# A graph network kernel whose adjacency-building stage takes its node blocks in another order

## The chip, the cores and the metric

The kernel runs on one core of one Trainium2 chip. The metric is device time in microseconds, as the median of several executions. The engines are TensorE (PE in the profile, with PEld its weight loads), VectorE (DVE), ScalarE (ACT), GpSimd (POOL) and SyncE (SP), which issues most of the DMAs.

## What is computed

A graph of 3125 nodes with 128 features and 100000 edges, sorted by destination, goes through four residual blocks, each followed by a layer norm. The last one distinguishes 8 types of edges (relations). Cut to what matters:

```
x = layernorm(x + gcn3(x))        # 3 layers: A-normalised sum over edges, W, layer norm, relu
x = layernorm(x + gcn1(x))        # sum over edges of x @ W.T + b
x = layernorm(x + gin(x))         # (1+eps)*x + sum over edges, two linear layers with batch norm
x = layernorm(x + rgcn2(x))       # 2 layers: per relation, mean over its edges, times W[r]

def rgcn_layer(x, src, dst, etype, W, W_root, b, num_rels):
    h = einsum('ni,rio->rno', x, W)
    msg = h[etype, src]
    seg = dst * num_rels + etype
    sums = segment_sum(msg, seg, N * num_rels)
    cnt = segment_sum(1, seg, N * num_rels)
    mean = sums / maximum(cnt, 1.0)
    return mean.reshape(N, num_rels, do).sum(axis=1) + x @ W_root + b
```

## The kernel before, in words

All sums over edges of the first three blocks are done as dense matrix products with the matrix of edge counts, 3200 x 3200, so the **first stage** builds this matrix from the list of edges. Everything after it uses the matrix. The nodes lie in 25 blocks of 128 (NB = 25), and two blocks make a superblock (SB = 13; the last one, 12, holds only block 24). For blocks 0 to 14 (ND = 15) the stage also builds one matrix of counts for each of the 8 relations, in bytes; for blocks 15 to 24 the last part of the kernel gathers rows by edge instead, so no such matrices are made. In what follows a block is *counted* if its relation matrices are built, and *plain* if not. Superblocks 0 to 6 are counted, 8 to 12 are plain, and superblock 7 holds counted block 14 and plain block 15.

The steps for a superblock s are, with the lines of the profile:

- `coarse` (L258): VectorE compares a sample of the destinations with the node numbers ("junk", L262), and makes row numbers ("crow", "irow", L265 and L266); POOL gathers two rows of the destinations ("g", L270).
- `search` (L277): VectorE counts in these ("junk", L281) and makes pointers into the list of edges ("ptr", L285).
- `fetch_edges` (L287): POOL gathers the edges of each node ("ew", L290).
- `keys` (L298): VectorE splits each edge into its fields ("f", "valid", "qf", "kb", "kq", L302 to L314), TensorE transposes the keys (L319) and ScalarE copies them to "kT" (L320).

For a block b, `total` (L344) goes through two halves. Each half makes one-hot matrices from kT on VectorE ("lo" and "hi", by the helper at L191), multiplies them on TensorE (L356) into the PSUM tile "bld", and ScalarE copies that to "at" (L359) in two copies. Between the halves stands `stored` of the block before. For a counted block each half goes on with `packed_counts` (L327): VectorE scales lo to "rlo" (L331) and makes "rhq" (L191); TensorE multiplies (L339), and ScalarE copies to "rb" in eight copies (L342). When both halves are done, eight DMAs store rb (L369, queue of SP).

`stored` (L375) adds the identity to at (VectorE, L376), stores it (adj_t, L377), transposes it on TensorE (L382), copies it to "av" on ScalarE in two copies (L383), stores that (adj, L384), and adds up degrees into "leave" on TensorE (L388), an accumulation that runs over all blocks.

The buffers lo, rlo, hi, rhq, at, rb and av exist twice each, ew three times, g six times; bld has two PSUM buffers.

The order of the work is written out in the loop at L404. The searches run ahead: while superblock s is built, between its two blocks, the keys of s + 1, the search and fetch of s + 2 and the coarse step of s + 3 are placed, and made to come after the last hi of the first block on VectorE (`behind`, L253). The framework gives each engine one list of instructions in a scheduled order: by the order of the program, but an instruction that is ready earlier can stand ahead of it. Each engine then runs its list in order.

```
for s in range(SB):
    built = total(2 * s, built)
    if s + 1 < SB:
        keys(s + 1, edges.pop(s + 1), last[0])
    if s + 2 < SB:
        search(s + 2, near.pop(s + 2), last[0])
        edges[s + 2] = fetch_edges(s + 2)
    if s + 3 < SB:
        near[s + 3] = coarse(s + 3, last[0])
    if 2 * s + 1 < NB:
        built = total(2 * s + 1, built)
stored(*built)
```

After the loop the degrees in leave become "dinv" (L424 to L438), and the **second stage** begins: x times dinv, split into two halves ("halves", L583 and L584), is multiplied with the matrix of counts. For each group of columns the matrix comes in five loads of five blocks each ("m", L594, queue of SP), is cast to "mf" by ACT (L611) or DVE (L613), and multiplied (L628). Beside this stage VectorE and POOL do small steps for the relations, among them a gather of edges ("gedge", L475).

The functions with their lines:

Of the kernel before, what the change touches and what calls it, by code (L numbers as in the profile page):

```python
# [24 lines left out]
NB = 25  # L25
# [20 lines left out]
def cols(m0, nb):  # L46
    return slice(m0 * P, (m0 + nb) * P)
# [8 lines left out]
SB = 13  # L56
# [3 lines left out]
ND = 15  # L60
# [13 lines left out]
def listed(ctx: ExitStack, tc: tile.TileContext, p: dict, out: bass.AP, bad):  # L74
# [92 lines left out]
    with tc.tile_pool(name="f_w", bufs=1) as wp, tc.tile_pool(name="f_bg", bufs=1) as bg:  # L167
# [28 lines left out]
        with tc.tile_pool(name="f_t1", bufs=1) as t1:  # L196
# [90 lines left out]
            def fetch_edges(s):  # L287
                ew = t1.tile([P, 2, SL], I32, name="ew", bufs=3)
                for i in range(2):
                    ld = nc.gpsimd.indirect_dma_start(  # L290
                        out=ew[:, i, :], out_offset=None, in_=pk[:],
                        in_offset=bass.IndirectOffsetOnAxis(ap=ptr[:, 2 * s + i : 2 * s + i + 1], axis=0),
                    )
                if s == 0:
                    packed.append(ld)
                return ew

# [77 lines left out]
            def stored(b, at):  # L375
                nc.vector.tensor_add(at[:, b, :], at[:, b, :], identb)  # L376
                nc.sync.dma_start(adj_t[b], at)  # L377
                av = t1.tile([P, NP], BF, name="av", bufs=2)
                for m0, nb in ((0, 13), (13, 12)):
                    t = psum.tile([P, 2048], BF, name="bld", tag="bld", bufs=2)  # L380
                    for k in range(nb):
                        nc.tensor.transpose(t[:, cols(k, 1)], at[:, m0 + k, :], identb)  # L382
                    nc.scalar.copy(av[:, cols(m0, nb)], t[:, : nb * P])  # L383
                nc.sync.dma_start(adj[b], av)  # L384
                for i in range(7):
                    w = min(512, NP - 512 * i)
                    q = 32 * (i % 4)
                    nc.tensor.matmul(leave[i // 4][q : q + 32, :w], onesb, av[:, 512 * i : 512 * i + w],  # L388
                                     start=(b == 0), stop=(b == NB - 1), skip_group_check=True)


            last = [None]
            near, edges = {}, {}
            built = None
            with tc.high_priority():
                near[0] = coarse(0)
                near[1] = coarse(1)
                search(0, near.pop(0))
                edges[0] = fetch_edges(0)
                key = keys(0, edges.pop(0))  # L400
            search(1, near.pop(1))
            edges[1] = fetch_edges(1)
            near[2] = coarse(2, key)
            for s in range(SB):  # L404
                built = total(2 * s, built)
                if s + 1 < SB:
                    keys(s + 1, edges.pop(s + 1), last[0])
                if s + 2 < SB:
                    search(s + 2, near.pop(s + 2), last[0])
                    edges[s + 2] = fetch_edges(s + 2)  # L410
                if s + 3 < SB:
                    near[s + 3] = coarse(s + 3, last[0])
                if 2 * s + 1 < NB:
                    built = total(2 * s + 1, built)
            stored(*built)

            tc.add_manual_dep(words.ins, started[0].ins.name, WAIT, reason="the search comes first")
# [336 lines left out]
    with until_end:  # L754
# [262 lines left out]
        with tc.tile_pool(name="f_hr", bufs=1, reuse_waits="tile") as hp:  # L1017
# [15 lines left out]
            for m0, nb in CH:  # L1033
                o = psum.tile([P, 512], F32, name="mi", tag="mi", bufs=2)
                for a in range(2):
                    nc.tensor.matmul(o[:, : nb * P], root2[:, a, :], hT[:, a, cols(m0, nb)],
                                     start=(a == 0), stop=(a == 1))
# [31 lines left out]
            for r in range(R):  # L1069
                nxt = None  # L1070
                for i, (m0, nb) in enumerate(DENSE):
                    inv = load_inv(r, m0, nb)
                    acc = relation(r, m0, nb, hr, work, 2.1, (1, 1, 1, 1, 1))
                    s = hp.tile([P, 512], F32, name="s", bufs=2)
# [628 lines left out]
```

## Time and profile before

| What | us |
|---|---|
| Time of three runs, median | 2020.77 (2017.62 to 2021.79) |
| Profiled execution | 2027.4 |
| its span, first to last instruction | 2025.5 |
| granted TensorE clock, mean | 0.975 |
| first lo of the first stage | 29.8 |
| last hi of the first stage | 389.1 |
| last av copy | 397.0 |
| first cast of the second stage | 404.35 |
| first product of the second stage | 407.85 |
| DVE busy, whole span | 1205.1 |
| ACT busy, whole span | 1253.0 |

The profile is one execution, recorded by the hardware. Its page cuts the span into 40 slices of 50.6 us and gives each engine's busy share in tenths. A *stretch* is the same between two times, in us. A *timeline* lists one engine's instructions: start, duration, engine, line, operation, output and inputs with their shapes, how often, and in brackets how long the engine had been idle and what released it. A *wait* names the engine and line that waited, and what for: us in total, how many times, and the longest. The profiled execution's own time is compared with its own sums; the median is of other executions.

### The profile page before, as it was taken

The numbers are of one execution on the slowest core, as the hardware profiler recorded it, in microseconds if no ns is written. First come the engines' busy times: TensorE is split into PE (matmuls) and PEld (weight loads), VectorE is DVE, ScalarE is ACT, GpSimd is POOL, SyncE is SP. The second block draws the span as 40 slices with busy tenths as digits, with TensorE's granted clock in tenths as the row PEclk, the third lists the DMA queues.
The fourth block names the chain that finished last, engine by engine and source line by source line (L and its number), as shares of the span: only waits on it lengthen the run. The fifth ranks groups of instructions, "written<-read, shape, count | busy, mean of one in ns | idle before, by whom it ended". The sixth has DMA issues, their size and how long they took to land.

```text
span 2025.5 us, 30183 instructions
## 1 busy us (share of the span) xinstructions
PE 1794.3 (89%) x11523; PEld 1387.0 (68%) x11523; DVE 1205.1 (59%) x2055; ACT 1253.0 (62%) x1118; POOL 859.5 (42%) x717
## 2 busy tenths in 40 slices
PE   2677676669999999889999999999999999999897
PEld 1555555458888888667577567758757777777676
DVE  6999998777768863475455345435346444434424
ACT  3999997757888666663233333233338777777774
POOL 5315624120000000027777267706716666666664
PEclk9999998889999999999999999999999999999998
DMA  4766776667888887477677457737659887888773
GB/s 100 277 271 266 291 287 237 247 189 232 255 259 257 251 268 235 140 225 190 177 212 207 148 171 209 188 101 198 184 151 269 243 228 220 235 240 245 196 204 101
DMA packets 398932, 435.67 MB, mean 215 GB/s; under 512 B 27166, under 2 KB 355838, under 8 KB 398776
## 3 DMA queue, kind: packets, MB, share of 16 engines
q1 hardware_dynamic: 346274, 336.92, 53.0%
q0 software_dynamic: 33632, 67.07, 12.9%
q10 hardware_dynamic: 18870, 29.66, 4.9%
q8 instruction: 92, 1.51, 0.3%
q14 instruction: 64, 0.52, 0.1%
HBM read 319.07 MB, written 114.46 MB: 214 GB/s over the span
## 4 chain that ended last, share of the span: by engine, by line
PE 57%; ACT 4%; issue 3%; DVE 3%; another core or an unknown queue 2%; DMA 1%; ACTq 0%; SPq 0%; DVEq 0%
PE acc L885 30%; PE acc L628 8%; PE x L927 8%; PE mi L962 4%; PE mi L975 4%; ACT m L767 3%; PE mi L966 1%; DMA back<-ht_d 1%; PE mi L650 0%; PE x L836 0%; PE mi L740 0%; DVE hilo L790 0%; ACT mf L611 0%; DVE f L1027 0%
## 5 line engine op out<-in xcount | busy, mean ns | idle before, releaser
L885 PE MATMUL acc<-m,hilo 128*128 128x512 f32 (+1 forms) x3200 | 792.3, 393 | 22.8 <-ACT m L767 10.8
L767 ACT CAST m<-m 128x2560 fp32r<-128x2560 uint8 (+1 forms) x225 | 486.8, 2196 | 372.5 <-PE acc L885 148.7
L885 PEld LDWEIGHTS acc<-m,hilo 128*128 128x128 f32 x3200 | 576.5, 190 | 130.3 <-issue 17.6
L919 POOL DMA_INDIRECT gx<-xt_d,gsrc x321 | 366.1, 1140 | 638.5 <-DVE z L1007 413.7
L919 POOL DMA_INDIRECT gx<-ht_d,gsrc x321 | 326.2, 1016 | 200.1 <-issue 72.0
L628 PE MATMUL acc<-mf,halves 128*128 128x512 f32 (+1 forms) x1750 | 383.9, 377 | 11.5 <-DVE mf L613 11.0
L628 PEld LDWEIGHTS acc<-mf,halves 128*128 128x128 f32 x1750 | 320.4, 190 | 60.4 <-DVE mf L613 11.9
L611 ACT CAST mf<-m 128x2560 fp32r<-128x2560 bf16 (+1 forms) x126 | 263.7, 2100 | 67.3 <-PE acc L628 34.8
L927 PE MATMUL x<-oh,gx 128*128 128x192 bf16 (+5 forms) x2208 | 227.1, 239 | 5.5 <-issue 5.2
L927 PEld LDWEIGHTS <-gx 128*128 128x128 bf16 x2208 | 157.0, 97 | 99.2 <-issue 89.6
L767 DVE CAST m<-m 128x2560 fp32r<-128x2560 uint8 (+1 forms) x95 | 158.5, 1670 | 110.6 <-issue 40.3
L909 DVE TENSOR_TENSOR oh<-iota,gkey 128x768 bf16<-128x768 bf16 (+1 forms) x170 | 90.3, 532 | 208.5 <-PE x L927 143.2
L342 ACT CAST rb<-bld 128x800 uint16<-128x800 f32 x240 | 180.0, 847 | 6.5 <-PE bld L339 6.5
L339 PE MATMUL bld<-rhq,rlo 128*128 128x200 bf16 x960 | 124.2, 253 | 49.4 <-ACT rb L342 36.5
L290 POOL DMA_INDIRECT ew<-pk,ptr x26 | 72.7, 2797 | 193.9 <-DVE ptr L285 189.6
L339 PEld LDWEIGHTS <-rlo 128*128 128x128 bf16 x960 | 86.9, 98 | 85.3 <-issue 80.9
L613 DVE CAST mf<-m 128x2560 fp32r<-128x2560 bf16 (+1 forms) x49 | 97.5, 1989 | 70.1 <-PE acc L628 69.9
L191 DVE TENSOR_TENSOR lo<-iota,kT 128x4096 bf16<-128x4096 bf16 x50 | 114.2, 2283 | 11.1 <-PE bld L356 11.1
L191 DVE TENSOR_TENSOR rhq<-iota,kT 128x6400 bf16<-128x6400 bf16 x30 | 104.4, 3480 | 0.0
L975 PE MATMUL mi<-wr,hT 128*128 128x512 f32 x200 | 93.4, 601 | 2.5 <-issue 1.6
L359 ACT CAST at<-bld 128x800 bf16<-128x800 f32 x100 | 79.4, 835 | 20.7 <-PE bld L356 20.6
L270 POOL DMA_INDIRECT g<-in_dst,irow x26 | 76.6, 2947 | 22.9 <-DVE crow L265 9.8
(238 smaller groups left out, 1624.4 us busy)
## 6 DMA issues: line engine op xcount, KB each, us to landing
m<-rel SPq DMA_DIRECT2D x240, 320.0 KB
rel<-rb SPq DMA_DIRECT2D x120, 400.0 KB
m<-adj SPq DMA_DIRECT2D x60, 640.0 KB
m<-adj_t SPq DMA_DIRECT2D x40, 640.0 KB
m<-adj SPq DMA_DIRECT2D x45, 480.0 KB
adj_t<-at SPq DMA_DIRECT2D x25, 800.0 KB
adj<-av SPq DMA_DIRECT2D x25, 800.0 KB
ht_d<-t SPq DMA_DIRECT2D x50, 384.0 KB
```

Of the source, the lines that this page charges most:

```text
L191: return nc.vector.tensor_tensor(o, (iota2 if of is None else of)[:, None, :width, :].to_broadcast([P, PU // 2, width, 2]), k[:, :, None, ...
L339: nc.tensor.matmul(pt[:, k, : R * NB], lo2[:, j // 2, :, j % 2], hq[:, j // 2, :, j % 2], start=True, stop=True)
L342: nc.scalar.copy(rb[:, :, j0 : j0 + 4], pt[:, :, : R * NB].rearrange("p j q -> p q j"))
L611: nc.scalar.copy(v, src)
L613: nc.vector.tensor_copy(v, src)
L628: nc.tensor.matmul(acc[:, :w], x[:, 5 * g + k, :], mf[:, k, :w], start=(g == 0 and k == 0 and i == 0), stop=(more is None and g == 4 and k ...
L767: casts_by[on_act] = nc.scalar.copy(v, src) if on_act else nc.vector.tensor_copy(v, src)
L885: nc.tensor.matmul(acc[:, :w], x[:, 5 * g + k, :], m[:, k, :w], start=(g == 0 and k == 0 and i == 0), stop=(g == 4 and k == 4 and i == 1),)
L909: ins = nc.vector.tensor_tensor(oh[:, : nt // 2], iota2[:, None, : GW * R, :].to_broadcast([P, nt // 2, GW * R, 2]), gkey[:, g, t : t + nt ...
L919: nc.gpsimd.indirect_dma_start(out=gx.rearrange("p i c -> p (i c)"), out_offset=None, in_=table[:], in_offset=bass.IndirectOffsetOnAxis(ap ...
L927: nc.tensor.matmul(acc[a // 512][:, a % 512 : a % 512 + z - a], gx[:, i, :], oh[:, t % 4 // 2, a - c0 : z - c0, t % 2], start=(a // 512 no ...
L975: nc.tensor.matmul(o, hT[:, a, cols(b, 1)], wr[:, a, r : r + 4, :].rearrange("p r c -> p (r c)"), start=(a == 0), stop=(a == 1))
```

## The change

The superblocks are taken in another order, `turns`, in which plain ones are spread between counted ones. With 8 superblocks up to 7 and 5 after it, the order is 0, 8, 1, 2, 9, 3, 10, 4, 5, 11, 6, 12, 7, and that of the blocks 0, 1, 16, 17, 2, 3, 4, 5, 18, 19, 6, 7, 20, 21, 8, 9, 10, 11, 22, 23, 12, 13, 24, 14, 15. The distances by which keys, search and coarse run ahead stay one, two and three superblocks, now counted in this order. No step is added or taken away. The accumulation in leave starts and stops with the first and last block of the new order.

```
-                if s == 0:
+                if s == turns[0]:
                     packed.append(ld)
...
-                                     start=(b == 0), stop=(b == NB - 1), skip_group_check=True)
-
+                                     start=(b == ORDER[0]), stop=(b == ORDER[-1]), skip_group_check=True)
+
+
+            most = (ND + 1) // 2
+            turns = sorted(range(SB), key=lambda s: ((s + 0.5) / most if s < most else (s - most + 0.6) / (SB - most), s))
+            ORDER = [b for s in turns for b in (2 * s, 2 * s + 1) if b < NB]
...
-                near[0] = coarse(0)
-                near[1] = coarse(1)
-                search(0, near.pop(0))
-                edges[0] = fetch_edges(0)
-                key = keys(0, edges.pop(0))
-            search(1, near.pop(1))
-            edges[1] = fetch_edges(1)
-            near[2] = coarse(2, key)
-            for s in range(SB):
+                near[0] = coarse(turns[0])
+                near[1] = coarse(turns[1])
+                search(turns[0], near.pop(0))
+                edges[0] = fetch_edges(turns[0])
+                key = keys(turns[0], edges.pop(0))
+            search(turns[1], near.pop(1))
+            edges[1] = fetch_edges(turns[1])
+            near[2] = coarse(turns[2], key)
+            for i, s in enumerate(turns):
                 built = total(2 * s, built)
-                if s + 1 < SB:
-                    keys(s + 1, edges.pop(s + 1), last[0])
-                if s + 2 < SB:
-                    search(s + 2, near.pop(s + 2), last[0])
-                    edges[s + 2] = fetch_edges(s + 2)
-                if s + 3 < SB:
-                    near[s + 3] = coarse(s + 3, last[0])
+                if i + 1 < SB:
+                    keys(turns[i + 1], edges.pop(i + 1), last[0])
+                if i + 2 < SB:
+                    search(turns[i + 2], near.pop(i + 2), last[0])
+                    edges[i + 2] = fetch_edges(turns[i + 2])
+                if i + 3 < SB:
+                    near[i + 3] = coarse(turns[i + 3], last[0])
                 if 2 * s + 1 < NB:
                     built = total(2 * s + 1, built)
```

## The prediction

> **What bounds the kernel now.** I began with the slices of the page. The chain of work that ended last is followed back only to 639 us, so it says nothing on the first stage (0 to 397 us); the stretches, the timelines of each engine and the waits must do that.
>
> ```profile
> DVE  6999998777768863475455345435346444434424
> ACT  3999997757888666663233333233338777777774
> PEclk9999998889999999999999999999999999999998
> ```
>
> ```profile
> 200.00:250.00 50.00, 34.80 (x446) 26.18 (x444) 46.77 (x48) 48.43 (x61) 32.97 (x7) 1.00 0.74 293
> 250.00:300.00 50.00, 35.19 (x451) 26.42 (x447) 48.27 (x55) 48.55 (x62) 9.81 (x4) 1.00 0.69 272
> 300.00:350.00 50.00, 31.69 (x525) 25.39 (x524) 42.00 (x80) 39.30 (x46) 17.98 (x10) 0.89 0.69 269
> 350.00:400.00 50.00, 34.38 (x575) 27.13 (x572) 36.27 (x51) 39.40 (x41) 10.57 (x8) 0.84 0.57 220
> ```
>
> A stretch's columns are the busy times of PE, PEld, DVE, ACT and POOL, then the granted clock, the DMA share and GB/s. Up to 300 us, while the counted blocks (0 to 14) are built, DVE and ACT are both full. From 300 to 390 us come the ten plain blocks; both engines have holes there, and the granted clock falls to 0.84 with the gaps of TensorE (which is not the bound; I count nothing for it). Counted work could fill these holes. How large are they? The waits of DVE up to 400 us answer:
>
> ```profile
> DVE lo L191 <- PE bld L356: 11.1, 7, 4.1
> DVE junk L281 <- DMA g<-in_dst,irow: 8.5, 4, 4.4
> DVE rlo L331 <- PE bld L339: 5.4, 4, 1.8
> ```
>
> (us in total, times, longest.) The middle line is the start, which stays as it is. The others are 11.1 us of DVE waiting to write the next "lo", all between 302 and 386 us, and 5.4 us before "rlo", from 175.9 us on. Between 51.6 us and its last "hi" (389.1 us) DVE waits for nothing else, and the change takes no work from it. So **16.5 us is the most that it can bring**; "holes" of 14 us in the last stretch look larger only because they hold the drain after 389 us.
>
> Both waits have one cause. A counted superblock costs DVE 34.9 us (51.6 to 86.5) and ACT 36.6 us (kT copies at 231.6 and 268.2), so ACT falls behind by about 1.7 us each time, until DVE's two buffers are full. At the one passage from counted to plain the whole lag is paid:
>
> ```profile
> 306.17 2.29 DVE L191 TENSOR_TENSOR lo<-iota,kT 128x4096 bf16<-128x4096 bf16 x1 [0.65 <-PE bld L356]
> ...
> 313.55 2.29 DVE L191 TENSOR_TENSOR lo<-iota,kT 128x4096 bf16<-128x4096 bf16 x1 [4.06 <-PE bld L356]
> ```
>
> ```profile
> 306.95 5.94 ACT L342 CAST rb<-bld 128x800 uint16<-128x800 f32 x8
> 312.82 1.56 ACT L359 CAST at<-bld 128x800 bf16<-128x800 f32 x2
> 314.62 2.89 ACT L383 COPY av<-bld 128x1664 bf16<-128x1664 bf16 x2 [0.24 <-PE bld L382]
> ```
>
> DVE ended its last counted operation at 298.50, ACT emptied its result at 312.8: 14.3 us behind, where 0.3 for the matmul and 5.9 for eight copies (6.2) would be the least. The lag is thus 8 us here.
>
> **The change, part by part.** Let R be the end of DVE's last "rhq" before a plain block, and L ACT's lag over that least.
>
> *Waits that go: -16.5 us.* A plain superblock costs DVE 16.4 us (four times lo 2.20 and hi 0.90, two small adds, 3.7 of keys, search and coarse) and ACT about 13.4 (eight "at" copies at 0.78, four "av" at 1.44, kT, gaps of 0.2 to 0.3). It gives back what one or two counted superblocks put in. With one plain after every one or two counted, L stays between 0 and about 3 instead of 8, so the "rlo" waits (all at full lag) should end, and the "lo" waits as they stand.
>
> *New passages: +3 us.* There are now four such passages with a search in the middle (after superblocks 0, 2, 3, 5) instead of one. The third "lo" of the plain pair needs the first used up, at R + 7 + L (298.5 + 7 + 8 = 313.5, which the trace shows); DVE gets there at R + 6.3 + 3.7 = R + 10. That is 3 us to spare, so the 3.7 us of search now cover it. The fourth "lo" and the add to "at" (L376) wait for ACT's second pair of "at" copies: R + 6.2 + L, plus 1.6, 3.1 (av with its gap) and 1.6, is R + 12.5 + L, and DVE is there at about R + 13.2. Each passage costs L - 0.7: nothing to 2 us. With L of 0, 2, 0 and 2 (a wait lowers the next L) this is 3; bounds 0 and 6.
>
> *Keys of the last turn: +5 us.* This is the price most easily overlooked. The keys of the next superblock are made between the two blocks of the current one, so the second block hides the way over PE's transposes and ACT's kT copy. Superblock 12 has only block 24, and in the new order superblock 7 comes after it. DVE ends its keys at R + 6.3 + 1.55 = R + 7.9, then has nothing to do until kT is there. ACT first empties the counted block (R + 6.2 + L), then "at" 1.6, "av" 3.1, and takes kT after the next "at": about R + 12.5 + L. Wait: 4.6 + L, 5 with L small. From below, at the start of the kernel, with nothing queued, keys that ended at 28.5 had kT at 29.3: 0.9 us. From above, both "at" pairs first and L = 2.5: 8 us. I take the value near the queue that the 312.82 rows show.
>
> *The drain: +2 us.* Before, block 24 follows nine plain ones, and from the last hi (389.1) to the last av (396.95) it takes 7.85 us. Now the end is counted 14, plain 15. With ACT at the least lag (the kT wait sees to that), R + 6.2 for the eight copies, then at 1.6, av 3.1, at 1.6, add and transposes 1.0, av 2.9 gives R + 16.4; DVE ends at R + 6.3, so the drain is 10.1. Bounds 0 and 5.
>
> *Stores of the last blocks: +1 us.* Relation stores of block 14 (8 x 400 KB) now go into SP's queue some 10 us ahead of the next stage's loads. With three stores of 800 KB that is 5.7 MB; the rows of 316 to 324 us moved 407 to 409 GB/s, so 14 us, to R + 20.5, against R + 16.4 for the last issue. The first load (640 KB) is some 4 us late at the queue. Before, it was issued at 397.53 and its cast began at 404.35, so most of that is hidden; if not, 4 us. The load for blocks 15 to 19 now waits for the last store, where it was that for blocks 20 to 24, one group later; same bound.
>
> *At nothing:* the choice of the start and stop block of "leave", the first fetch, and the numbers of matmuls, copies, gathers and stores, which are the same. At the start superblock 0 stays first and the searches are alike.
>
> Sum: -16.5 + 3 + 5 + 2 + 1 = **-5.5 us**. The profiled execution took 2027.4 us (span 2025.5), so 2022 there; it lies 6.6 us above the median shown, and from 2020.8 I get **2015.3 us**. Nothing after 397 us changes in itself: it all waits for "dinv", which needs every block.
>
> **The rivals.** *It comes to nothing (chance 0.32).* ACT's work on the counted blocks (36.6 per superblock) is the true bound there, and new waits at the passages eat the rest: with the passages and the kT wait at their upper ends and the drain as reckoned, 6 + 8 + 2 = 16, the time is 2020. For it: two pairs of counted superblocks stay together. Against it: DVE was without waits from 51.6 to 175 us, while ACT fell behind.
>
> *More than forecast (0.14).* The order of execution differs from that of the program wherever something is ready early (a "lo" runs ahead of the keys at 321.76), so kT may be copied at once and the passages may cost nothing: -16.5 + 1 + 0 + 2 + 0 = -13.5, 2007.
>
> *Slower (0.12): the gathers come late.* A turn's search reads what POOL gathered in the turn before.
>
> ```profile
> 192.60 2.74 POOL L290 DMA_INDIRECT ew<-pk,ptr  x1 [14.38 <-DVE ptr L285]
> 195.65 9.07 POOL L290 DMA_INDIRECT ew<-pk,ptr  x1 [0.30 <-issue]
> 205.03 6.90 POOL L270 DMA_INDIRECT g<-in_dst,irow  x1 [0.30 <-issue]
> 212.23 1.69 POOL L270 DMA_INDIRECT g<-in_dst,irow  x1 [0.30 <-issue]
> ...
> 328.01 1.44 POOL L290 DMA_INDIRECT ew<-pk,ptr  x1 [17.49 <-DVE ptr L285]
> 329.75 2.17 POOL L290 DMA_INDIRECT ew<-pk,ptr  x1 [0.30 <-issue]
> ```
>
> Beside counted blocks four gathers take 21.3 us, and 2 more to land (47.8 to 49.8 at the start). Counted turns are 35 us apart, so this is hidden. Next to a plain superblock the distance is one counted block, one plain block and the search: 15.6 + 6.3 + 3.7 = 25.6, of which 23.5 lie between ptr and the next search. Margin 0.2 us. There are eight such turns. Over 26 us for the four (the longest of each kind seen: 2.74, 9.07, 8.74, 5.35 and gaps), every turn that begins beside a counted block, four of them, waits 5 us: +20, 2035 in sum; it turns slower from 2.4 us each. Against it: half of such a turn is plain work, and beside that the four took 8 us (328.01 to 336.3).
>
> Rows first, a rule beside them: the Trainium skill (GPSIMD Engine Reference, section 1, Specifications) says that GpSimd's way to SBUF contends with VectorE instructions that have two SBUF inputs. That is what lo and hi are, so by the rule plain blocks would not relieve the gathers, and the sum would be that of this rival. The short gathers at 328 us beside lo and hi speak against it here.
>
> **How the numbers follow.** A measurement of this kernel can tell some 0.2%, 4 us, from no change. Forecast, -4 to -9 us: 0.42; more than that: 0.14; so faster 0.56. Within 4 us: 0.32. Slower: 0.12. The range runs from the fast rival (2007) to just past no change (2023); outside lie most of the slower case and a little below.
>
> **What would show it.** In the profile after, "rlo" waits gone; "lo" waits below 8 us, one of them of some 5 us before the "lo" of block 14, its releaser the kT copy or a plain gap; the last av copy near 391 to 392 us; the first cast of "mf" 7 to 8 us behind it. Waits of "junk" for g or of "f" for ew in mid-stage would be the gathers. I am wrong if ACT shows new gaps in counted superblocks, or if DVE's waits sum to 16 us again in other places.

## The result and the profile after

The changed kernel took 2029.0 us in the median of nine runs (2025.72 to 2036.29); nine runs of the kernel before, on the same chip, had a median of 2021.79 (2013.51 to 2027.0). The ratio is 1.0061, with a 95% interval of 1.0043 to 1.008. It is slower, by 9 to 16 us by this interval. The two medians alone lie 7 us apart (1.0036), so the size is less certain than the sign; a second pair on another chip, below, gave 1.0054. The forecast was 5.5 us faster.

One caution about the two profiles. The profiled execution of the kernel after took 2026.06 us (span 2024.2, clock 0.974). That of before took 2027.4, more than any of the nine runs of before, so these two spans must not be subtracted. Nor do the two profiles start alike: ScalarE's last copy for block 1 ends at 74.4 us in the one and at 71.1 in the other, though superblock 0 comes first in both. Both kernels were therefore run again side by side on another chip (called A below; `orig_order` is the old order, `after_again` the changed one). There the spans are 1964.3 and 1976.9 us, and this pair shows where the time goes:

| us, chip A | old order | changed | difference |
|---|---|---|---|
| last copy to rb of block 1 (ScalarE) | 71.39 | 71.70 | +0.31 |
| last hi of VectorE | 384.29 | 388.14 | +3.85 |
| last av copy of ScalarE | 392.13 | 401.87 | +9.74 |
| first cast of the second stage | 399.33 | 410.25 | +10.92 |
| last product of the second stage | 828.1 | 838.9 | +10.8 |
| span | 1964.3 | 1976.9 | +12.6 |

On this chip the loss is made in the first stage and carried unchanged through the second. In the first pair of profiles the last av is only 4.2 us later (401.2 and 397.0), but counted from the last copy of block 1 the stage takes 330.1 us instead of 322.5, 7.6 more (chip A: 330.2 and 320.7, 9.4 more). So one asks what the first stage looks like now. First the slices of the page:

```profile
DVE  6999999578778863375355445535336433444424
ACT  3898898856887765663233333333338777778774
PEclk9999999978999999999999999999999999999999
```

and the stretches that were shown of before (busy times of PE, PEld, DVE, ACT, POOL, then clock, DMA share, GB/s):

```profile
200.00:250.00 50.00, 33.40 (x486) 25.93 (x483) 46.99 (x68) 43.73 (x53) 23.81 (x9) 0.93 0.65 258
250.00:300.00 50.00, 35.10 (x434) 26.25 (x434) 49.92 (x48) 48.64 (x61) 24.43 (x6) 1.00 0.71 278
300.00:350.00 50.00, 34.20 (x498) 26.68 (x495) 46.09 (x63) 44.37 (x54) 24.32 (x8) 0.93 0.64 242
350.00:400.00 50.00, 34.18 (x480) 26.67 (x480) 31.64 (x30) 45.44 (x56) 6.46 (x4) 0.97 0.67 269
```

The change does spread the work: ACT's 39 us of busy time in the last two stretches are now 44 to 45, and the granted clock is not below 0.93 in these four (the slices show 7 and 8 behind them, from 405 to 506 us, where the second stage begins). But ACT has holes in the second, fourth and fifth slices now (8 where there was a 9), and in the stretch from 200 us (43.73 where it had 48.43). The holes have moved, they have not been filled. The waits of DVE, up to 410 us (us in total, times, longest), say the same in figures:

```profile
DVE at L376 <- ACT at L359: 12.7, 6, 9.8
DVE lo L191 <- PE bld L356: 11.5, 5, 3.2
...
DVE rhq L191 <- ACT kT L320: 2.2, 2, 2.1
```

The 9.8 is the end of the stage, after the last hi. Without it there are 2.8 + 11.5 + 2.2 = 16.5 us of waits inside the stage, as much as before (11.1 + 5.4). The rlo waits are gone, and everything they were worth stands at other places. One of these places, the passage from counted block 11 to plain block 22, on VectorE and on ScalarE:

```profile
293.48 3.49 DVE L191 TENSOR_TENSOR rhq<-iota,kT 128x6400 bf16<-128x6400 bf16 x1
296.88 2.29 DVE L191 TENSOR_TENSOR lo<-iota,kT 128x4096 bf16<-128x4096 bf16 x1
299.09 0.99 DVE L191 TENSOR_TENSOR hi<-iota,kT 128x1600 bf16<-128x1600 bf16 x1
303.31 2.29 DVE L191 TENSOR_TENSOR lo<-iota,kT 128x4096 bf16<-128x4096 bf16 x1 [3.23 <-PE bld L356]
```

```profile
302.56 1.57 ACT L359 CAST at<-bld 128x800 bf16<-128x800 f32 x2
304.03 5.95 ACT L342 CAST rb<-bld 128x800 uint16<-128x800 f32 x8
```

VectorE ends its last rhq at 296.88; ScalarE ends the copies of it at 309.98. That is 13.1 us, and 6.2 would be the least, so the lag L of the prediction is 6.9 us here. It had been forecast at 0 to 3.

And the end of the stage. The eight copies of the last rhq (which ends at 379.97) and what must follow them:

```profile
384.86 5.94 ACT L342 CAST rb<-bld 128x800 uint16<-128x800 f32 x8
390.73 1.56 ACT L359 CAST at<-bld 128x800 bf16<-128x800 f32 x2
392.53 2.89 ACT L383 COPY av<-bld 128x1664 bf16<-128x1664 bf16 x2 [0.24 <-PE bld L382]
...
398.29 2.89 ACT L383 COPY av<-bld 128x1664 bf16<-128x1664 bf16 x2 [1.04 <-PE bld L382]
```

The copies begin 4.9 us after the rhq, where 0.3 was the least: L is 4.6, and the last av comes 13.7 us after the last hi, where it was 7.85 before.

### The profile page after: what moved, and what is told of

It is laid out like the page before. It is cut to its first block, busy times and chain, and to the rows that moved or that the text cites. A ratio compares the mean times of both kernels' runs of the same rounds, so it can differ in the third digit from the quotient of the medians.

```text
span 2024.2 us, 30154 instructions
## 1 busy us (share of the span) xinstructions
PE 1799.1 (89%) x11523; PEld 1392.9 (69%) x11523; DVE 1206.5 (60%) x2055; ACT 1253.5 (62%) x1118; POOL 862.2 (43%) x717
## 4 chain that ended last, share of the span: by engine, by line
PE 57%; ACT 3%; issue 2%; DVE 2%; another core or an unknown queue 1%; DMA 1%; ACTq 0%; DVEq 0%
PE acc L889 31%; PE x L931 8%; PE acc L632 7%; PE mi L966 4%; PE mi L979 4%; ACT m L771 2%; DMA back<-ht_d 1%; PE mi L970 1%; PE mi L654 0%; DVE hilo L794 0%; PE mi L744 0%; ACT mf L615 0%; PE x L840 0%; PE acc L739 0%
## 5 line engine op out<-in xcount | busy, mean ns | idle before, releaser
L632 PEld LDWEIGHTS acc<-mf,halves 128*128 128x128 f32 x1750 | 322.0, 191 | 59.7 <-DVE mf L617 9.3
L342 ACT CAST rb<-bld 128x800 uint16<-128x800 f32 x240 | 181.2, 845 | 12.8 <-PE bld L339 12.4
L339 PE MATMUL bld<-rhq,rlo 128*128 128x200 bf16 x960 | 128.9, 261 | 46.5 <-ACT rb L342 34.1
L290 POOL DMA_INDIRECT ew<-pk,ptr x26 | 83.0, 3191 | 178.0 <-DVE ptr L285 140.2
L339 PEld LDWEIGHTS <-rlo 128*128 128x128 bf16 x960 | 89.4, 100 | 82.9 <-issue 75.4
L191 DVE TENSOR_TENSOR lo<-iota,kT 128x4096 bf16<-128x4096 bf16 x50 | 114.2, 2285 | 11.5 <-PE bld L356 11.5
L359 ACT CAST at<-bld 128x800 bf16<-128x800 f32 x100 | 79.8, 838 | 18.4 <-PE bld L356 13.7
L356 PE MATMUL bld<-hi,lo 128*128 128x50 bf16 x1600 | 59.9, 191 | 23.3 <-DVE hi L191 10.0
```

Source lines behind the costliest of these rows:

```text
L191: return nc.vector.tensor_tensor(o, (iota2 if of is None else of)[:, None, :width, :].to_broadcast([P, PU // 2, width, 2]), k[:, :, None, ...
L339: nc.tensor.matmul(pt[:, k, : R * NB], lo2[:, j // 2, :, j % 2], hq[:, j // 2, :, j % 2], start=True, stop=True)
L342: nc.scalar.copy(rb[:, :, j0 : j0 + 4], pt[:, :, : R * NB].rearrange("p j q -> p q j"))
L632: nc.tensor.matmul(acc[:, :w], x[:, 5 * g + k, :], mf[:, k, :w], start=(g == 0 and k == 0 and i == 0), stop=(more is None and g == 4 and k ...
```

## The experiments

Five chips (A to E) were used, and the kernel before ran on each. On A, B and C the kernel before takes 1967.6 to 1969.0 us in the median, on D and E 2019.6 to 2020.1. Each ratio is against the kernel before on its own chip, and positions in the stage are compared between A, B and C, or between D and E, only. "Waits" is the sum of VectorE's waits between 52 us and its last hi. "From block 1" is the time from ScalarE's last copy to rb of block 1 to the last av: it leaves out the start, which ends anywhere from 71.0 to 75.0 us in these profiles, also for one and the same order. The expectations give positions as on A to C; on D the old order's last av is at 397.6 instead of 392.1, so that some 5 us have to be added there.

| run (chip) | median us | ratio (95%) | last hi | last av | from block 1 | waits |
|---|---|---|---|---|---|---|
| orig_order (A) | 1968.67 | 1.0001 (0.9992 to 1.001) | 384.3 | 392.1 | 320.7 | 14.7 |
| after_again (A) | 1979.58 | 1.0054 (1.0041 to 1.0068) | 388.1 | 401.9 | 330.2 | 17.0 |
| in_turn (A) | 1977.11 | 1.0042 (1.0028 to 1.0055) | 387.7 | 400.2 | 328.8 | 16.9 |
| at3 (A) | 1968.92 | 1.0005 (0.9996 to 1.0014) | 378.0 | 392.4 | 320.2 | 6.4 |
| at3_before (B) | 1966.69 | 0.9996 (0.9986 to 1.0007) | 382.7 | 390.5 | 318.5 | 12.4 |
| end_plain (B) | 1975.38 | 1.003 (1.0018 to 1.0042) | 391.9 | 399.7 | 328.3 | 21.1 |
| at3_end (B) | 1971.3 | 1.0007 (0.9998 to 1.0016) | 383.8 | 391.7 | 317.9 | 10.7 |
| adjt_act (B) | 1993.09 | 1.0121 (1.0106 to 1.0137) | 406.1 | 417.9 | 343.9 | 32.5 |
| saved_after (C) | 1981.69 | 1.0063 (1.0046 to 1.008) | 389.6 | 403.3 | 330.1 | 16.1 |
| adjt_first (C) | 1979.45 | 1.0055 (1.004 to 1.0071) | 392.0 | 405.7 | 330.7 | 17.8 |
| at3_two (C) | 1963.59 | 0.9974 (0.9963 to 0.9984) | 382.5 | 390.3 | 316.9 | 10.5 |
| lo3_before (C) | 1963.68 | 0.9988 (0.9975 to 1.0) | 379.3 | 388.9 | 316.5 | 9.1 |
| keys_held (D) | 2027.04 | 1.0048 (1.003 to 1.0066) | 388.0 | 399.5 | 327.3 | 16.9 |
| keys_before (D) | 2022.1 | 1.0012 (0.9996 to 1.0028) | 389.8 | 397.6 | 324.8 | 19.1 |
| keys_two (D) | 2016.03 | 0.9982 (0.9967 to 0.9998) | 388.0 | 395.9 | 322.0 | 16.0 |
| two_groups (D) | 2019.27 | 0.9993 (0.9974 to 1.0011) | 387.0 | 394.8 | 322.7 | 16.8 |
| keys_end (E) | 2020.62 | 1.0003 (0.9986 to 1.0021) | 389.5 | 398.0 | 323.9 | 16.4 |
| lo3_two (E) | 2019.39 | 0.9997 (0.998 to 1.0014) | 388.5 | 397.4 | 323.3 | 16.6 |

### Where the loss is made

**after_again**: the changed kernel as it is. 

> The changed kernel as it is, for the size of the loss and its place. In its first profile the last av copy ended at 401.2 us against 397.0 before, and every later landmark up to 1520 us was 4 to 5 us later than before. Stage theory (the loss is made in the first stage alone): last av copy at 401 to 402 again, and the time 0.2 to 0.3% over the kernel before. Later theory (more is lost after the first stage): the same 401, but the time 0.5% or more over before, and a later landmark (the last product of L632, at 839.3 in the first profile against 835.2) further back than 4 us.

**orig_order**: the changed code with the old order.

```
-            turns = sorted(range(SB), key=...)
+            turns = [0, 1, 2, 3, 4, 5, 6, 7, 8, 9, 10, 11, 12]
```

> The new code with the turns 0, 1, 2 ... 12, so that it does what the kernel before does. Both theories: last av copy at 397, ratio 1.000. It tells how far two profiles and two medians of one and the same work lie apart: if the ratio is off by more than 0.002, differences of that size mean nothing here.

The rewritten loop costs nothing by itself (1.0001); the order alone does. The table of the pair above shows that 10.9 of the 12.6 us stand at the first cast and no more at the end of the second stage. So the place is that of the stage theory; the size that it gave, 0.2 to 0.3%, was half of the 0.54% measured. The last av of the old order stands at 392.1 and not at 397; 3.0 of these 5 us are the start.

**in_turn**: in the trace of the changed kernel the first rhq of the next counted turn runs ahead of the plain superblock's second block (310.69 us, while that block's lo and hi are still to come). Here it is held behind the hi of its own half.

```
+                if u == 0 and b > 0 and ORDER[ORDER.index(b) - 1] >= ND:
+                    behind(counts, last[0])
```

(`counts` is the instruction that makes rhq.)

> The changed kernel, but the first rhq of a counted superblock after a plain one has to stand behind its own hi on VectorE, so it can't run ahead of the plain superblock's second block. List theory (the schedule's reordering starves ACT: four gaps of 1.2 to 1.4 us before the at copies of the second plain block, while DVE makes 3.7 us of search and 3.4 us of rhq): these gaps end and the last av copy comes at 396 to 398. Drain theory (the loss is ACT's lag when the counted block 14 stands next to last): unchanged, 401. Store theory (ACT waits for the store of at): unchanged or a little later, the 4.5 us of waits for the store stay.

1.0042 and a last av 1.7 us earlier: the rhq that runs ahead is a small part at most, and the interval overlaps that of after_again.

### The buffers of "at"

Three savings of memory (one junk and one f buffer instead of two, rs in the slot of smf) make room for a third `at` buffer. **at3**: the changed order with it.

```
-                at = t1.tile([P, NB, P], BF, name="at", bufs=2)
+                at = t1.tile([P, NB, P], BF, name="at", bufs=3)
```

> The changed kernel with a third buffer for at (room made by fewer buffers for small tiles that only VectorE uses, which changes no order on PE and ACT). Store theory (the four waits of the at copies on the store of at, 4.5 us in sum, are a loss of ACT, which sets the end): the waits go, last av copy at 397 to 398, time 0.2% less than the changed kernel. List and drain theories: the waits go but reappear as waits for PE, last av copy at 400 to 401.

The whole loss is gone, 9.5 us at the last av, more than either theory had, but no gain is left over: although VectorE's waits fall from 17.0 to 6.4 us and its last hi comes 10.2 us earlier, ScalarE ends where it did in the old order (392.4 and 392.1). **at3_before**: the old order with it.

> The kernel before with the third buffer for at, made room for in the same way. The new order with this buffer ran 0.5% faster than without (1968.9 against 1979.6 us), as fast as before. Store theory (the new order makes plain blocks follow counted ones, and then at has to wait for a store that stands behind the 3.3 MB of relation stores): the old order has one such passage, so the buffer brings at most a fifth of what it brings the new order, 0 to 2 us, ratio 0.999 to 1.000. General theory (the buffer helps any order, and the new order's loss is something else): 5 us or more, ratio 0.9975 or less.

1.6 us at the last av, and 0.9996. So the third buffer is not a gain for this kernel in general, it mends something of the new order. **saved_after** is the control, with the savings but two buffers:

> The changed kernel with the three savings of memory that make room for the third at buffer (one junk and one f buffer instead of two, rs in the slot of smf), but with two at buffers as before. The lists of TensorE and ScalarE are those of the changed kernel. Theory (the third at buffer itself takes the loss away): nothing changes, 1.005 to 1.006 of the kernel before, last av at 401 to 402. Rival (the savings move VectorE's small steps and that did it): 1.000 to 1.003, last av at 392 to 397.

1.0063: the savings do nothing. ScalarE's waits on the store of at in the changed kernel ("ACT at L359 <- DMA adj_t<-at" has 4.5 us, before had none) suggested that the buffer is held by its store, which stands in SP's queue behind eight relation stores of 400 KB. Two runs moved that store. **adjt_act** issues it from ScalarE:

```
-                nc.sync.dma_start(adj_t[b], at)
+                nc.scalar.dma_start(adj_t[b], at)
```

> The changed kernel with two buffers for at, but its store adj_t issued from ACT's queue, so that it doesn't stand behind the relation stores of SP's queue. Store theory (it is the place in the queue that keeps at busy): the loss goes as with the third buffer, last av copy 5 to 9 us earlier than the changed kernel's, less what 25 issues cost ACT. Buffer theory (two buffers are too few whatever the queue, since at is also held by the transposes): gain below 3 us; ACT's waits then name PE, or VectorE's add to at, ahead of the store.

A miss for every theory: 1.0121, and the last av 16 us later than in after_again. The issue stands in ScalarE's own list, behind an add that VectorE makes, and VectorE's waits nearly doubled, to 32.5. It says nothing on the queue. **adjt_first** leaves the issuer alone and puts the relation stores behind it (in `stored` instead of at the end of `total`); TensorE's and ScalarE's lists stay the same, instruction by instruction.

```
 nc.sync.dma_start(adj_t[b], at)
+if b < ND:
+    for r in range(R):
+        nc.sync.dma_start(rel[r][b]..., rb...)
```

> The changed kernel, but the eight stores of the relation matrices of a block are issued behind the store of its adj_t instead of ahead of it; the lists of TensorE and ScalarE stay those of the changed kernel. Theory A (at is held by its store, which stands behind 3.3 MB in SP's queue; what the records show as waits on that store, 4.5 us, is what it costs directly, the rest is in the lists): the waits of at on adj_t go, last av 397 to 398.5, 1.003 to 1.004. Theory B (the store costs nearly all): last av 392 to 394, 1.000 to 1.0015. Theory C (the wait on the store hides other waits that take its place): last av 400 to 402, 1.0045 to 1.006.

1.0055: nothing is gained, and the waits on that store are 4.5 us as before. In after_again these waits are 0.4 us in all, and the loss is there. The theory that the store's place in the queue makes the loss falls.

### The end of the stage

**end_plain**: the last two turns exchanged, so that plain block 24 is last again and the drain short.

```
-            turns = sorted(range(SB), key=...)
+            turns = [0, 8, 1, 2, 9, 3, 10, 4, 5, 11, 6, 7, 12]
```

> The changed kernel with the last two turns exchanged, 7 before 12, so that the last two blocks are plain (15, 24), as before, and no keys stand between blocks 24 and 14. Drain theory (6 us of the loss is ACT's lag at the end, 13.8 us from the last hi to the last av against 7.8): drain back to 8 to 10 us, last av copy 4 to 6 us earlier than in the changed kernel (396 to 398 on the chip where that had 401.9), ratio to before 1.002 to 1.003. Copies theory (ACT sets the end, and the drain only shows its lag): DVE's last hi moves later by as much as the drain shrinks, last av copy within 2 us of the changed kernel's, ratio 1.004 to 1.006.

The drain does shrink (7.8 us instead of 13.7), but the last hi comes 3.7 us later, and only 2.2 of the 9.7 us come back at the last av, close to the copies theory. The ratio, 1.0030, is that of the drain theory, so the run does not settle how much of the loss is the drain's. **at3_end**, the same end with the third buffer:

> The third buffer for at and the last two turns exchanged (7, then 12). With the third buffer alone the last hi ended at 378.0, 6 us before that of the old order (384.3), and the last av at 392.4, a drain of 14.4 us. Drain theory: the drain goes to 8 to 10, last av at 386 to 388, ratio to before 0.997 to 0.998, the best so far. Copies theory: last av at 391 to 393, ratio 1.000.

No gain in time on at3 (1.0007 against 1.0005 on chip A), as the copies theory said: the last av is at 391.7 instead of 392.4, though from block 1 the stage is 2.3 us shorter.

### TensorE's list

What did the third buffer change, if the store was not the matter? The lag answers. L, taken as in the prediction, at the last half of some counted blocks:

| block | 1 | 2 | 5 | 7 | 8 | 11 |
|---|---|---|---|---|---|---|
| old order (orig_order, A) | 0.4 | 2.9 | 3.7 | 5.3 | 7.9 | 6.7 |
| changed (after_again, A) | 0.4 | 5.4 | 5.5 | 5.8 | 7.0 | 6.7 |
| at3 (A) | 0.5 | 0.4 | 2.3 | 3.7 | 4.3 | 4.9 |
| end_plain (B) | 0.5 | 5.9 | 5.5 | 6.5 | 6.7 | 6.7 |
| keys_held (D) | 1.0 | 3.1 | 4.1 | 1.6 | 2.2 | 2.9 |
| keys_end (E) | 0.8 | 2.8 | 3.6 | 1.7 | 3.4 | 4.4 |
| two_groups (D) | 0.9 | 3.5 | 4.2 | 6.0 | 0.5 | 2.5 |

In the changed order a plain superblock lies between blocks 1 and 2. It was to lower L by up to 3 us; L goes up by 5, where in the old order, without the plain superblock, it goes up by 2.5. Both engines' rows just there, of the changed kernel (after_again, TensorE, then ScalarE):

```profile
95.74 0.52 PE L339 MATMUL bld<-rhq,rlo 128*128 128x200 bf16 x4 [0.21 <-ACT rb L342]
98.90 0.43 PE L319 MATMUL mi<-identb,kb 128*128 128x128 bf16 x2 [2.64 <-DVE kb L314]
99.30 0.23 PE L319 MATMUL mi<-identb,kq 128*128 128x128 bf16 x1
99.37 0.56 PE L339 MATMUL bld<-rhq,rlo 128*128 128x200 bf16 x4
99.73 0.86 PE L356 MATMUL bld<-hi,lo 128*128 128x50 bf16 x16
```

```profile
92.67 4.47 ACT L342 CAST rb<-bld 128x800 uint16<-128x800 f32 x6 [0.22 <-PE bld L339]
99.96 0.83 ACT L342 CAST rb<-bld 128x800 uint16<-128x800 f32 x1 [2.81 <-PE bld L339]
100.68 0.48 ACT L320 COPY kT<-mi 128x384 bf16<-128x384 bf16 x1
```

TensorE's list has the transposes of the next turn's keys (L319) among the matmuls of the counts of the first half (L339). VectorE has not yet made those keys, since they come after the whole block in its own list. TensorE stands still for 2.64 us with matmuls behind it whose inputs are ready, and ScalarE for 2.81. The same stands twice more in this profile, 1.70 us before the transposes at 188.55 us and 2.03 before those at 243.31. (In in_turn only the first of the three is left, and there the last av came 1.7 us earlier.) In at3 the first place reads

```profile
96.11 0.57 PE L356 MATMUL bld<-hi,lo 128*128 128x50 bf16 x16 [0.21 <-ACT rb L342]
96.84 0.57 PE L356 MATMUL bld<-hi,lo 128*128 128x50 bf16 x16 [0.16 <-ACT rb L342]
97.71 1.14 PE L339 MATMUL bld<-rhq,rlo 128*128 128x200 bf16 x8 [0.29 <-DVE rhq L191]
98.85 0.43 PE L319 MATMUL mi<-identb,kb 128*128 128x128 bf16 x2
```

The transposes stand behind the matmuls at L356 of both halves, and nobody waits for the keys. So there were two explanations left: the place of the transposes in the list, or the two buffers themselves. **keys_held** keeps two buffers and fixes the place.

```
-    nc.tensor.transpose(t[:, cols(i, 1)], k, identb)
+    behind(nc.tensor.transpose(t[:, cols(i, 1)], k, identb), lastmm[0])
```

(`lastmm` is the last matmul at L356.)

> The changed kernel with the transposes of the next keys held, in TensorE's list, behind the second half's matmuls (L356) of the first block of the turn; two at buffers. (1) The list makes the loss: ScalarE's lag behind the counted block of the third turn (block 2) falls from 5.4 to between 0 and 1 us, as with the third buffer, last av 392 to 396, 1.000 to 1.002. (2) The two buffers make it: the stall of 2.8 us at 97 to 100 us goes, but waits of at or lo take its place; last av 399 to 402, 1.004 to 1.006.

The lag does come down, to between 1.3 and 5.0 us from block 2 on. But at block 2 it is 3.1 us, not the 0 to 1 of (1). From ScalarE's last copy of block 1 to that of block 2 it takes 34.3 us, against 37.6 in after_again and 32.0 in at3. So of the 5.6 us that the third buffer saves there, 3.3 come from the place of the transposes, and 2.3 stay with the two buffers, or with what else differs in the lists. Of these, 1.7 show as a wait for the store of an earlier `at` (the row of keys_end, below, which has 1.74 there):

```profile
89.43 1.55 ACT L359 CAST at<-bld 128x800 bf16<-128x800 f32 x2 [1.74 <-DMA adj_t<-at]
```

The last av, 399.5, lies in the range of (1) with the 5 us of this chip added (397 to 401). But the time hardly follows: 1.0048, in the range of (2). In the profile the stage has become shorter (from block 1 327.3 us, against 330.2 in after_again and 324.8 in the old order on D), but the profiled execution took 2016.29 us, 10.8 below the median of the twelve, and where the rest of the loss lies stays open. VectorE's waits are 16.9 us as ever, and they stand at new places again, with the times in total, number and longest:

```profile
DVE at L376 <- ACT at L359: 16.3, 5, 7.6
DVE junk L281 <- DMA g<-in_dst,irow: 10.2, 5, 4.2
```

Of the 16.3, the last 7.6 is the drain; another 7.2 is one wait, in the last turn:

```profile
355.89 0.98 DVE L191 TENSOR_TENSOR hi<-iota,kT 128x1600 bf16<-128x1600 bf16 x1
...
365.73 0.22 DVE L376 TENSOR_TENSOR at<-at,identb 128x128 bf16<-128x128 bf16 x1 [7.18 <-ACT at L359]
366.12 2.29 DVE L191 TENSOR_TENSOR lo<-iota,kT 128x4096 bf16<-128x4096 bf16 x1 [0.16 <-ACT kT L320]
```

This is the wait that the prediction had named, for the keys of counted block 14, which have no second block before them to hide behind. And 3.8 us of the junk waits (2.4 and 1.3, at 306 us) are the late gathers, in one turn. **keys_before** holds the transposes in the old order:

> The order of before, with the transposes of keys held in the same way. There ScalarE is behind anyway when TensorE comes to the transposes, so they cost nothing: last av 391 to 392.5, 0.9995 to 1.0005, by (1) and (2). If they cost the old order too: last av 387 to 390, 0.998 to 0.999.

1.0012, not told from no change. In the old order the place of the transposes does not matter: in the profile of orig_order TensorE waits for keys only four times after 52 us, 0.35 us each, and all among the plain blocks at the end. **keys_end** joins keys_held and the order of end_plain, and so takes away both the lag and the wait for the last keys:

> Transposes held, two at buffers, the changed order but for its end: 6, 7, 12 instead of 6, 12, 7. If the lag from TensorE's list and the wait for the last keys are the whole loss: the wait of 7 us is gone, the drain is 7.8, last av 8 us or more below that of the changed kernel, 0.999 to 1.001. If single plain superblocks between counted ones cost with two buffers beyond that: waits of at, lo and adj_t of 6 us or more stay at the passages, 1.002 to 1.004.

1.0003 (0.9986 to 1.0021): no loss can be measured, with two `at` buffers and plain superblocks still singly between counted ones. The last av (398.0) is where the old order had it on such a chip (397.6 in keys_before; from block 1 323.9 and 324.8). Apart, the two edits left 1.0048 and 1.003, from block 1 327.3 and 328.3. With the lag, the wait for the last keys is mostly covered (2.1 us in the changed kernel); without the lag it is bare (7.2). The expectation's other signs held only in part. The last av is not 8 us but 3.2 below that of the changed kernel's first profile. Waits of 16.4 us remain, among them 4.1 for kT in the last turn, which is superblock 12 here. ScalarE's waits for the store of `at` remain too, 5.0 us, so they are not enough to make a loss that can be measured. The loss is accounted for within that interval; a gain is nowhere.

### Fewer passages, more lo

**at3_two**: third buffer, and the plain superblocks in two groups, `turns = [0, 1, 2, 3, 8, 9, 4, 5, 6, 7, 10, 11, 12]`.

> Third at buffer and the order 0 to 3, 8, 9, 4 to 7, 10, 11, 12: two passages instead of five, and three plain superblocks at the end. If each passage costs, also with three buffers (ScalarE's lag of 5 to 7 us is met at every one): last av 388 to 390.5, 0.998 to 0.9995. If ScalarE's work alone sets the end, whatever the order: last av 391 to 393, 1.000 to 1.001, as with the spread order.

0.9974 (0.9963 to 0.9984): faster than the kernel before, clear of the noise. With the same buffer and single plain superblocks, at3_end had 1.0007, so the grouping does it. Its profile places 3.8 us of the gain in the first stage (from block 1 316.9 against 320.7 in the old order on A; at the last av 1.8); where the rest of the 5.4 us between the medians is, stays open. The same order without the third buffer, **two_groups**, and with the transposes held, **keys_two**:

> The order 0 to 3, 8, 9, 4 to 7, 10, 11, 12, nothing else changed (two at buffers, transposes as the framework puts them). The list behind the plain pair has the transposes where the version with the third buffer has them, so by (1) last av 390 to 392, 0.9975 to 1.000. By (2) 393 to 397, 1.0005 to 1.0025.

> Transposes held, two at buffers, order 0 to 3, 8, 9, 4 to 7, 10, 11, 12. (1): as with the third buffer in that order (390.3), last av 389 to 391.5, 0.997 to 0.9995. (2): the two buffers cost at the second passage, last av 393 to 397, 1.0005 to 1.0025.

0.9993 and 0.9982: no loss with two buffers, the ratios and (with the 5 us added) the last av as in (1), and no difference between the two that stands clear of their intervals. Two plain superblocks in a row do give the lag back (6.0 at block 7, 0.5 at block 8 in the table), which one alone did not in the changed kernel; VectorE pays 8 us of waits for that at the passage. **lo3_before** gives the old order a third lo, **lo3_two** gives it to the two groups:

```
-                    lo = t1.tile([P, PU // 2, P, 2], BF, name="lo", bufs=2)
+                    lo = t1.tile([P, PU // 2, P, 2], BF, name="lo", bufs=3)
```

> The order of before with a third lo buffer (same savings of memory). VectorE's waits for lo, 9.7 us there, were what the change wanted to take away. If they cost the end of the stage anything: last av 386 to 389 instead of 392, 0.997 to 0.9985. If ScalarE's copies set the end and VectorE's waits only show it: hi (two buffers) or the PSUM buffers stop VectorE instead, last av 390.5 to 392, 0.9995 to 1.0005.

> Third lo buffer (same savings of memory), order 0 to 3, 8, 9, 4 to 7, 10, 11, 12, two at buffers. If the third lo and the two passages add up (lo3_before 0.9988, at3_two 0.9974): 0.996 to 0.998, last av some 4 us below the old order's. If they answer the same waits: 0.998 to 0.9995.

In the old order VectorE's lo waits (9.7 us) turn into 6.1 us of waits for hi, its last hi comes 5 us earlier, and the last av 3.3 us earlier (chips A and C): 0.9988 (0.9975 to 1.0). VectorE's waits as a whole fall by 5.6 us there, from 14.7 to 9.1. In at3 they are 8.3 us below the old order's and the last av is where it was. So what the waits that the change went after are worth at the end of the stage differs with the way in which they go, from nothing to some 3 us here. The two do not add up (0.9997); that profile has a wait of 3.9 us for late edges (f for ew at 374 us), one execution's.

## Why the prediction was wrong

Step by step, as the prediction put them; the right column is the changed kernel's first profile, or the pair on chip A where it says so.

| step | forecast (bounds) | measured |
|---|---|---|
| waits that go | -16.5 | the rlo waits go (0 to 0.7 left); 16.5 us of waits stand elsewhere |
| new passages | +3 (0 to 6) | 11.5 (lo) + 2.8 (at) = 14.3 |
| keys of the last turn | +5 (0.9 to 8) | 2.1; 7.2 in keys_held |
| drain | +2 (0 to 5) | +5.9 (13.7 less 7.85; the same on chip A) |
| stores of the last blocks | +1 (0 to 4) | +1.2 on chip A (first cast 8.4 behind the last av, 7.2 before) |

**The step that failed** is the reason under the first line: "It gives back what one or two counted superblocks put in. With one plain after every one or two counted, L stays between 0 and about 3 instead of 8." The durations were right, but their sum was not the time that ScalarE takes. Instead of the 13.4 us forecast for a plain superblock, the first one took 19.5: from its last copy of block 1 to that of block 2 it needs 37.6 us in after_again and 18.1 in orig_order, where no plain superblock lies between. So L was 5.4 to 7 at the passages behind it, not 0 to 3. With three `at` buffers it takes 13.9 (32.0 less the 18.1 of at3_before), the number forecast. VectorE's 16.4 was 17.0. What was missing was the order within an engine's list: the forecast took each instruction as done when its inputs and its engine are free, and looked at what a *program order* would do. But the framework had made another list, in which early transposes hold up TensorE and, through it, ScalarE; with them held back the same stretch takes 34.3 us, 3.3 less. Another 2.3 us stay with the two buffers of `at`, for which the prediction has no term: with three they go.

**Passages** then follow from L: the prediction's own formula, L - 0.7 each, gives 4.8 to 6.2 us at L = 5.5 to 6.9; measured were 2.4 to 3.8 us at each of four (behind superblocks 2, 3, 5 and 6: lo 1.91, 2.43, 3.23 and 2.96, and adds of 0.3 to 0.6), 0.5 at the first, where L was still 0.4, and 1.0 at the end. With the true L the formula would have been too high, with L of 0 and 2 it was far too low. **The drain** was reckoned with L = 0 ("the kT wait sees to that"), as R + 16.4; it came at R + 21.2, and 4.6 of the 4.8 us between are the L of the last rows shown above. **The keys of the last turn** cost less than forecast since the lag covered them; in keys_held, with the lag down, they cost 7.2, near the upper bound. So the terms pull against each other: with a small L the wait for kT is long, with a large L the passages and the drain are.

**The sum** on chip A: +3.8 at the last hi, of which 2.3 are VectorE's waits (17.0 less 14.7) and 1.5 stay unplaced; +5.9 of drain; +1.2 behind it: 10.9 us at the first cast, and as much at the last product of the second stage. The remaining 1.8 us of the spans' difference stay open.

**Signs that were named.** "I am wrong if ACT shows new gaps in counted superblocks, or if DVE's waits sum to 16 us again in other places": both happened, the gap of 2.81 us at 97 us and the 16.5. The last av was to be at 391 to 392 and came at 401.2.

**Rivals.** "It comes to nothing" (0.32) came nearest: ScalarE's work on the counted blocks sets the end, and new waits eat the rest. Its sum of 16 (6 + 8 + 2) is close to what was measured by another split (14.3 + 2.1, then the drain), and it ends on zero only because it stopped the drain at 2. at3 fits its premise best: VectorE's waits are 8.3 us less than in the old order (6.4 and 14.7), and ScalarE ends at the same time (392.4 and 392.1). But ScalarE's copies alone do not set the end either, since lo3_before has the same copies and ends at 388.9. 16.5 us was a bound that none of the runs came near. The range, 2007 to 2023, held the late gathers for the only way to the slower side. "Slower" (0.12) was for those: in the changed kernel no search in mid-stage waits for them, in keys_held one turn does, with 3.8 us.

The Trainium skill (Perfetto Trace Analysis, Optimization Strategy) says that where a kernel has several regimes with different most-contended engines, interleaving them may improve performance. That is this change. Here interleaving one by one gave 1.0061, and in coarser groups, with a third `at` buffer, 0.9974: the runs agree with it in the second form only.

**What stays open.** Why the framework's list with two `at` buffers has the transposes early is not known; that it has them early was read off the profile. The third buffer seems to act both through the list and as a buffer (3.3 and 2.3 us at the first passage); the list of at3 was not run with two buffers, and the waits of at on adj_t were in no run taken away alone. keys_end and end_plain, which differ in the transposes alone, ran on chips of different speed, and their intervals overlap by a little (1.0021 and 1.0018); the interval of keys_end by itself leaves room for a loss of 4 us. The granted clock of the executions goes with their time: in keys_held 0.980 with 2016.29 us and 0.968 with 2038.06. How much of what the profiles do not place lies there is open.

## What to carry to other kernels

Before mixing two kinds of work so that one fills the other's holes, find out whether the engine that the other waits for has any room: here VectorE's waits were visible (16.5 us), but runs that took 5.6 and 8.3 us of such waits away ended 3.3 us earlier and not at all, since ScalarE was nearly as full (48 of 50 us beside counted blocks). A change of order is also a change of every engine's instruction list; look in the profile for an instruction that waits for another engine while ready ones stand behind it (TensorE's key transposes), because such a stall of 3 us keeps up a lag that the other kind of work was to take away (5.4 us instead of 0.4 at block 2 here). And try larger groups beside the finest interleaving: with three `at` buffers, pairs of plain superblocks gave 0.9974 and single ones 1.0007.

## What the runs showed of the hardware that was not expected

The same gathers of 128 rows took from 0.94 to 10.13 us. In the changed kernel four of them beside a counted block took 20.6 us from first to last:

```profile
191.47 2.74 POOL L290 DMA_INDIRECT ew<-pk,ptr  x1 [13.63 <-DVE ptr L285]
194.51 9.07 POOL L290 DMA_INDIRECT ew<-pk,ptr  x1 [0.30 <-issue]
203.89 6.89 POOL L270 DMA_INDIRECT g<-in_dst,irow  x1 [0.30 <-issue]
211.09 0.95 POOL L270 DMA_INDIRECT g<-in_dst,irow  x1 [0.30 <-issue]
```

In at3 the same four, also beside a counted block, took 10.4 us (from 190.74 on), and none from 139 us on was longer than 3.96. The prediction put the long ones down to counted blocks; what makes them long is not settled. A DMA issued from ScalarE's list (adjt_act) cost the stage 16 us although one issue is shown with 0.33 us, 25 of them 8. What the issue waits for, and the lists that changed with it, may make the rest; the two were not told apart.
